# Adding chunk 1 onto chunk 0 for the first block of nodes alone, with twelve tile buffers and GpSimd making layer 1's sender column

## The chip, the cores and the metric

The kernel runs on one core of a Trainium2 chip. The metric is the device time of one execution in microseconds (us). A core has a matrix engine (TensorE, PE in the profile; its weight loads are PEld), three engines for elementwise work (VectorE, DVE; ScalarE, ACT; GpSimd, POOL) and an engine that here only issues DMAs (SyncE, SP). Each engine runs its own list of instructions in order. Where an instruction needs another engine's result, it waits on a semaphore.

## The reference

64 graphs of 256 nodes with 128 features go through four layers; every layer first normalises the rows (layer norm, then ReLU) and adds its result to its input. All of it is float32. The four layers are a pairwise attention (layer 0), a message network with a sigmoid edge weight (layer 1), a dense attention (layer 2) and a gated recurrence of five steps (layer 3). The change touches layer 0 and one column of layer 1:

```python
# layer 0, per graph: W1, W2 are the two halves of adj
s1 = jnp.einsum('bkf,ef->bke', x, W1)
s2 = jnp.einsum('bkf,ef->bke', x, W2)
pre = s1[:, :, None, :] + s2[:, None, :, :] + b_lin
h = jnp.where(pre >= 0, pre, ALPHA * pre)          # ALPHA = 0.2
e = jnp.einsum('bije,e->bij', h, a) + bias         # bias = adj
attn = jax.nn.softmax(e, axis=2)
out = jax.nn.sigmoid(jnp.einsum('bij,bjf->bif', attn, x))
# layer 1
x_h = jax.nn.elu(x @ Wi + bi)
a_src = x_h @ We[:H, 0]
a_tgt = x_h @ We[H:, 0]
e = jax.nn.sigmoid(a_tgt[:, :, None] + a_src[:, None, :] + be[0])
```

For each of the 256 x 256 pairs of nodes of a graph, layer 0 takes a leaky ReLU of 256 sums and their dot product with `a`. That is 64 x 256 x 256 x 256 elements, and it is most of the kernel's work.

## The kernel before

**The pair tiles.** A node i and a chunk `ec` (128 of the 256 entries of `a`) give one tile of 128 partitions (entries of the chunk) x 256 elements (nodes j): the larger of `s2` and minus `s1` of node i. Eight such tiles form a *batch* in a buffer `r` of 128 x 4 x 2 x 256: four groups `g` of 32 nodes by two blocks `ic` of 128 nodes, all for one row t (node `ic*128 + 32*g + t`). The buffers rotate; `BUFS = 11` of them exist. TensorE then multiplies each group of a batch with a window of signs, `a_win`, whose column t selects the row of the output, and sums into `e_ps`, which has the logits of a graph: four matmuls of 512 columns in the program, each on its own 32 columns of the array, so that the four run beside each other. A float32 matmul is two passes in the profile, so a batch is eight MATMUL records.

**Who makes the tiles.** Three engines do, by one line each. VectorE makes four or eight tiles in one instruction (L669, 128x1024 or 128x2048). ScalarE makes one per instruction (L687), and GpSimd one per instruction (L692).

**Merging.** The entries of `a` are sorted by sign and scaled by their absolute value into the weights, so that chunk 0 and chunk 1 have the same sign in each partition, but for one partition at most. So TensorE need not multiply both chunks: VectorE can add chunk 1 of a tile onto its chunk 0 (L709, one instruction that takes the maximum and adds), which is a *merge*. It spares the making of that tile for chunk 1 and TensorE's work on it. A row that is merged needs 8 tiles, 8 merges and one batch; a row that is not needs 16 tiles and two batches. The odd partition is set right by `left2`, `left_w` and `left_b`: `senders` puts a bounded row onto the `adj` bias, for both blocks (`adj_l`, L570), and the softmax adds it (L755).

**What sets the order.** The instruction lists are written by a planner in the kernel (`Model`, `Chain`, and the loop at the end). It keeps a planned time per engine, adds a cost for each instruction (a tile costs ScalarE 365 ns and GpSimd 454, a merge 392, a batch on TensorE 858), and always emits what could start first. Other layers come as chains of steps that interleave with the tiles of the next graphs: `ahead` (layer norm and projections of the next graph), `behind` (softmax of the last graph), `chain12` (layers 1 and 2), `chain3` and later ones (layer 3). `Pairs.begin` decides on a merge by the planner's count: a row is merged where at least `SPARE = 5` finished batches wait for TensorE. The order is fixed when the program is built; the chip runs it with semaphores.

**Groups.** Graphs go in pairs (`GROUPS`: 30 groups of two and four of one). `load_x` fetches a group's input through SyncE into one of five buffers, three groups ahead.

**Layer 1's sender column.** `y_ps` has 129 columns per block, the last being `x_h @ We`. ScalarE copies the first 128 to `y` (L855), and VectorE makes `a_src` of the last out of PSUM, once a graph (L857). The tanh of the edge weights (L875, ScalarE) reads `a_src`.

Of the kernel before, what the change touches and what calls it, by code (L numbers as in the profile page):

```python
# [8 lines left out]
F32 = mybir.dt.float32  # L9
# [3 lines left out]
P = 128  # L13
N = 256
# [4 lines left out]
INV_SQRT_D = 1.0 / (128.0 ** 0.5)  # L19
BUFS = 11  # L20
SPARE = 5
# [34 lines left out]
def kernel(ctx: ExitStack, tc: tile.TileContext, ins: dict, out: bass.AP):  # L56
# [71 lines left out]
    def load_x(g):  # L128
        xt = ap.tile([P, 2 * GROUPS[g], P], F32, tag="xt", name="xt", bufs=5)
        nc.sync.dma_start(out=xt, in_=of_group(x, g))  # L130
        return xt
# [76 lines left out]
    biases = {k: column("L3_gnn_" + k) for k in ("w3_b", "u3_b", "w4_b", "w5_b", "u5_b")}  # L208
    xts.append(load_x(2))

# [9 lines left out]
    def constants0():  # L220
# [32 lines left out]
        dve(2).tensor_tensor(place, dif, neg_pl, ALU.add)  # L253

        last, a_abs1 = col("last"), col("a_abs1")
        dve(2).tensor_scalar(last, place, n_pos, None, ALU.is_equal)
        dve(2).tensor_tensor(a_abs1, a_abs, last, ALU.mult)
        dve(2).tensor_tensor(a_abs1, a_abs, a_abs1, ALU.subtract)
        perm = lent([P, 2, 2, P], "perm", "e_t", 2)
        for src in range(2):  # L260
            for c, size in ((0, a_abs), (1, a_abs1)):
                dve(P).tensor_scalar(
                    perm[:, src, c, :], places[:, c, :], place[:, src : src + 1],
                    size[:, src : src + 1], ALU.is_equal, ALU.mult,
                )
# [43 lines left out]


        odd = constant([P, 1], "odd")
        dve(1).tensor_scalar(odd, p_two[:, 1:2], n_pos, None, ALU.is_equal)
# [7 lines left out]
        dve(2).tensor_tensor(left, a_col, last, ALU.mult)  # L320
        dve(2).tensor_scalar(left, left, odd_all, 0.8, ALU.mult, ALU.mult)
        dve(2).tensor_scalar(left_n, left, -1.0, None, ALU.mult)
# [107 lines left out]
    def ln_relu(space, xt, tag, ln, when=None, at=None):  # L430

        G = xt.shape[1]
        for g in range(G):
            if g % 2 == 0:
                yield "dve", when, at
            if g == 0:
                st = sp.tile([P, G, 6], F32, tag=tag + "_st", name="bst", bufs=2)
                mv = sp.tile([P, G, 2], F32, tag=tag + "_mv", name="bmv", bufs=2)
            dve(P).bn_stats(st[:, g, :], xt[:, g, :])
        yield "dve"  # L440
        for g in range(G):
            dve(6, more=15).bn_aggr(mv[:, g, :], st[:, g, :])
        yield "pool"

        ve = sp.tile([P, G], F32, tag=tag + "_ve", name="bve", bufs=2)
        minus = sp.tile([P, G], F32, tag=tag + "_mm", name="bmm", bufs=2)
        pool(277).tensor_scalar(ve, mv[:, :, 1], 1.0, LN_EPS, ALU.mult, ALU.add)
        pool(150).tensor_scalar(minus, mv[:, :, 0], -1.0, 0.0, ALU.mult, ALU.add)
        rstd = sp.tile([P, G], F32, tag=tag + "_rs", name="brs", bufs=2)
        pool(1085).tensor_tensor(rstd, ve, neg_half[:, 0:G], ALU.pow)  # L450
        shift = sp.tile([P, G], F32, tag=tag + "_sh", name="bsh", bufs=2)
# [81 lines left out]
    def bounds(of):  # L533
# [11 lines left out]
        yield "act"  # L545
        rows = sp.tile([P, P], F32, tag="rows", name="rows", bufs=2)
        act(P, 1).activation(
# [10 lines left out]
    def senders(b, of, to):  # L558

        h_t = flat(of["h_t"][:, 2 * b : 2 * b + 2, :])  # L560
        if "bound" not in of:
            yield from bounds(of)
        yield "pe", settled
        p = psum_h([P, N], "left_ps")
        mm(p, lhsT=left2, rhs=h_t, start=True, stop=True)
        for ic in range(2):
            yield "dve", None, of["bound_at"]
            if ic == 0:
                adj_l = ap.tile([P, 2, N], F32, tag="adj_l", name="adj_l", bufs=3)
            dve(N, 1).scalar_tensor_tensor(  # L570
                adj_l[:, ic, :], p, of["bound"][:, 2 * b + ic : 2 * b + ic + 1], adj_n[:, ic, :],
                ALU.min, ALU.add,
            )
# [12 lines left out]
    class Pairs:  # L586

        def __init__(self, g, b, of, snd):
            self.g, self.b, self.of, self.snd = g, b, of, snd
# [8 lines left out]
                "p c (k g t) -> p c g k t", k=2, g=4  # L601
            )

        def more(self):
# [39 lines left out]

        def nodes(self, t, g2):

            return [
                (g, ic, self.b * N + ic * P + 32 * g + t)
                for g in (2 * g2, 2 * g2 + 1) for ic in range(2)
            ]  # L650

        def make(self, who):
# [10 lines left out]
            if who == "dve":  # L663
                whole = g2 == 0 and self.todo and self.todo[0][0] is batch
                if whole:
                    self.todo.pop(0)
                n = 4 if whole else 2
                model.op("dve", model.WHOLE if whole else model.HALF)
                nc.vector.tensor_tensor(  # L669
                    r[:, 2 * g2 : 2 * g2 + n, :, :],  # L670
                    s2[:, ec : ec + 1, :].unsqueeze(1).to_broadcast([P, n, 2, N]),
                    self.s1n_v[:, ec, 2 * g2 : 2 * g2 + n, :, t : t + 1].to_broadcast([P, n, 2, N]),
                    ALU.max,
# [7 lines left out]
            else:  # L681
                for g, ic, i in self.nodes(t, g2):
                    if g > 2 * g2 or ic:
# [17 lines left out]
        def merge(self):  # L701

            _, batch, g2 = self.merges.pop(0)
            r, t = batch["r"], batch["t"]
            for g, ic, i in self.nodes(t, g2):
                if g > 2 * g2 or ic:
                    yield
# [22 lines left out]
        def multiply(self):  # L730
# [7 lines left out]
            model.op("pe", model.BATCH)  # L738
            for g in range(4):
                nc.tensor.matmul(  # L740
                    self.e_ps[bass.ts(g, 32), :, :].rearrange("p a b -> p (a b)"),
                    lhsT=a_win[:, batch["ec"], 31 - t : 63 - t], rhs=flat(r[:, g, :, :]),
                    start=False, stop=self.over, skip_group_check=True,
                )

    def softmax0(g, b, of, e_ps, snd):
# [87 lines left out]
    def layer1(x1):  # L834
# [8 lines left out]
        for b in range(NB):  # L843
# [11 lines left out]
            act(N).copy(y[:, bass.ts(b, 2), :], y_ps[:, :, 0:P])  # L855
            yield "dve"
            dve(2, 1).tensor_scalar(  # L857
                a_src[:, bass.ts(b, 2)], y_ps[:, :, P], 0.5, be_h, ALU.mult, ALU.add
            )
        yield "pool"  # L860
        x1b = bp.tile([P, G, P], F32, tag="x1b", name="x1b")
        counts["x1"] += 1
# [33 lines left out]
        for b in range(NB):  # L896
            for jc in range(2):
                mm(
                    rc_ps[:, bass.ts(b, N)], lhsT=y[:, b * 2 + jc, :], rhs=e_ts[b][:, jc, :],
                    start=(b == 0 and jc == 0), stop=False, skip_group_check=True,  # L900
                )
# [387 lines left out]
```

## Time and profile before

| What | us |
|---|---|
| time, median of 3 runs | 5038.96 (5033.29 to 5039.40) |
| profiled execution, its own time | 5032.98 |
| span of its profile, first to last instruction | 5031.1 |
| PE busy | 4975.7 |
| PEld busy | 1949.9 |
| DVE busy | 4926.9 |
| ACT busy | 4945.2 |
| POOL busy | 4817.0 |
| last merge on DVE ends at | 4936.5 |

Busy time is the union of an engine's instructions. On PE it says little by itself: a MATMUL record of 512 columns is some 593 ns long, while a set of four starts every 430 ns, so records overlap and cover gaps. What an engine can do at most is better read from the starts of instructions that follow each other without a wait. DMA is busy for 2% of the time, and the granted TensorE clock is 0.999 of full speed.

### The profile page before, as it was taken

The numbers are of one execution on the slowest core, as the hardware profiler recorded it, in microseconds if no ns is written. First come the engines' busy times: TensorE is split into PE (matmuls) and PEld (weight loads), VectorE is DVE, ScalarE is ACT, GpSimd is POOL, SyncE is SP. The second block draws the span as 40 slices with busy tenths as digits, with TensorE's granted clock in tenths as the row PEclk, the third lists the DMA queues.
The fourth block names the chain that finished last, engine by engine and source line by source line (L and its number), as shares of the span: only waits on it lengthen the run. The fifth ranks groups of instructions, "written<-read, shape, count | busy, mean of one in ns | idle before, by whom it ended". The sixth has DMA issues, their size and how long they took to land. (4 is left out here: it accounts for less than half of the span.)

```text
span 5031.1 us, 151796 instructions
## 1 busy us (share of the span) xinstructions
PE 4975.7 (99%) x57307; PEld 1949.9 (39%) x57307; DVE 4926.9 (98%) x9026; ACT 4945.2 (98%) x12984; POOL 4817.0 (96%) x10725
## 2 busy tenths in 40 slices
PE   9999999999999999999999999999999999999998
PEld 3334433333334333343333333333333443333433
DVE  9999999999999999999999999999999999999995
ACT  8999999999999999999999999999999999999995
POOL 8999999999999999999999999999999999999991
PEclk9999999999999999999999999999999999999999
DMA  0000000000000000000000000000000000000000
GB/s 23 4 5 2 5 6 6 6 2 6 6 6 6 2 6 6 6 6 2 6 6 6 6 2 6 6 6 6 4 6 6 6 4 3 5 4 4 4 4 8
DMA packets 56017, 28.02 MB, mean 6 GB/s; under 512 B 20336, under 2 KB 55280, under 8 KB 55280
## 3 DMA queue, kind: packets, MB, share of 16 engines
q1 hardware_dynamic: 54736, 18.04, 1.5%
q8 instruction: 449, 7.36, 0.6%
q14 instruction: 288, 2.36, 0.2%
q10 hardware_dynamic: 544, 0.26, 0.0%
HBM read 9.84 MB, written 8.45 MB: 4 GB/s over the span
## 5 line engine op out<-in xcount | busy, mean ns | idle before, releaser
L692 POOL TENSOR_SCALAR r<-s,s1n 128x256 f32<-128x256 f32 x10100 | 4567.7, 476 | 55.7 <-PE e_ps L740 28.0
L687 ACT ACTIVATE r<-s_act,s 128x256 f32<-128x256 f32 x9736 | 4360.0, 1073 | 4.6 <-PE e_ps L740 4.3
L740 PE MATMUL e_ps<-r,a_win 128*32 128x512 f32 x27824 | 3251.8, 593 | 8.8 <-DVE r L709 4.0
L669 DVE TENSOR_TENSOR r<-s_ps,s1n 128x2048 f32<-128x2048 f32 (+1 forms) x1210 | 2120.7, 1790 | 0.8 <-POOL r L692 0.8
L709 DVE SCALAR_TENSOR_TENSOR r<-s_ps,s1n,r 128x256 f32<-128x256 f32 x4944 | 2013.3, 471 | 0.2
L740 PEld LDWEIGHTS e_ps<-r,a_win 128*32 128x32 f32 x27824 | 918.8, 110 | 1721.4 <-issue 1290.3
L687 ACT ACTIVATE r<-s,s 128x256 f32<-128x256 f32 x512 | 318.8, 1234 | 0.0
L458 ACT ACTIVATE h<-x,bsh,brs 128x128 f32<-128x128 f32 x384 | 264.3, 1040 | 10.5 <-POOL bsh L452 5.0
L109 PE MATMUL m_ps<-adj_t,hn 128*32 128x256 f32 x4096 | 253.6, 381 | 1.1 <-ACT hn L1066 1.1
L1025 ACT ACTIVATE m_ps<-gate_ps,br 128x512 f32<-128x512 f32 (+1 forms) x170 | 194.7, 1145 | 14.2 <-PE gate_ps L109 13.1
L1045 ACT ACTIVATE hv_ps<-hv_ps,bh 128x512 f32<-128x512 f32 (+1 forms) x170 | 198.7, 1169 | 7.2 <-PE hv_ps L109 7.2
L1043 ACT ACTIVATE gate_ps<-gate_ps,bz 128x512 f32<-128x512 f32 (+1 forms) x170 | 203.8, 1200 | 1.1 <-PE gate_ps L109 1.1
L1015 ACT COPY m_t<-m_ps 128x512 f32<-128x512 f32 (+1 forms) x170 | 193.9, 1140 | 6.1 <-PE m_ps L109 5.6
L109 PEld LDWEIGHTS m_ps<-adj_t,hn 128*32 128x32 f32 x4096 | 140.0, 110 | 126.2 <-issue 46.1
L109 PE MATMUL gate_ps<-m_t,t_w_w 128*32 128x512 f32 (+1 forms) x1360 | 172.7, 572 | 2.6 <-ACT m_t L1015 2.2
L109 PE MATMUL gate_ps<-m_t,w_t 128*32 128x512 f32 (+1 forms) x1360 | 172.5, 568 | 2.5 <-ACT m_ps L1025 2.4
L109 PE MATMUL hv_ps<-rh,u_th 128*32 128x512 f32 (+1 forms) x1360 | 172.1, 567 | 2.1 <-DVE rh L1028 2.0
L109 PE MATMUL hv_ps<-m_t,t_w_w 128*32 128x512 f32 (+1 forms) x1360 | 172.4, 568 | 0.0
L1066 ACT COPY hn<-hn_ps 128x512 f32<-128x512 f32 (+1 forms) x136 | 153.2, 1127 | 8.7 <-PE hn_ps L116 8.6
L109 PE MATMUL gate_ps<-hf,u_t 128*32 128x512 f32 (+1 forms) x1088 | 141.9, 571 | 0.0
L109 PE MATMUL s_ps<-h0t,w_p 128*32 128x256 f32 (+1 forms) x1568 | 136.2, 446 | 1.2 <-ACT h0t L474 0.5
L450 POOL TENSOR_TENSOR brs<-bve,neg_half 128x4 f32<-128x4 f32 (+1 forms) x136 | 133.5, 982 | 0.0
(214 smaller groups left out, 4781.2 us busy)
## 6 DMA issues: line engine op xcount, KB each, us to landing
xt<-in_x_dram SPq DMA_DIRECT2D x30, 256.0 KB
out_dram<-y SPq DMA_DIRECT2D x30, 256.0 KB
row<-rows SPq DMA_DIRECT2D x128, 0.5 KB
xt<-in_x_dram SPq DMA_DIRECT2D x4, 128.0 KB
out_dram<-y SPq DMA_DIRECT2D x4, 128.0 KB
bound<-row SPq DMA_DIRECT2D x30, 2.0 KB
raw_L_gnn_w_w<-in_L_gnn_w_w_dram SPq DMA_DIRECT2D x3, 128.0 KB
adj_n<-in_adj_dram ACTq DMA_DIRECT2D x1, 256.0 KB
```

Of the source, the lines that this page charges most:

```text
L109: nc.tensor.matmul(out[bass.ts(c, 32), :], lhsT=lhsT[:, bass.ts(c, 32)], rhs=rhs, **flags)
L458: act(P, 2, 1).activation(h[:, g, :], xt[:, g, :], AF.Relu, bias=shift[:, g : g + 1], scale=rstd[:, g : g + 1],)
L669: nc.vector.tensor_tensor(r[:, 2 * g2 : 2 * g2 + n, :, :], s2[:, ec : ec + 1, :].unsqueeze(1).to_broadcast([P, n, 2, N]), self.s1n_v[:, ec ...
L687: nc.scalar.activation(r[:, g, ic, :], s2[:, ec, :], AF.Relu, bias=s1[:, ec, i : i + 1])
L692: nc.gpsimd.tensor_scalar(r[:, g, ic, :], s2[:, ec, :], FLT_MAX, s1n[:, ec, i : i + 1], ALU.min, ALU.max,)
L709: nc.vector.scalar_tensor_tensor(r[:, g, ic, :], self.own("dve")[:, 1, :], self.of["s1n"][:, 1, i : i + 1], r[:, g, ic, :], ALU.max, ALU.add,)
L740: nc.tensor.matmul(self.e_ps[bass.ts(g, 32), :, :].rearrange("p a b -> p (a b)"), lhsT=a_win[:, batch["ec"], 31 - t : 63 - t], rhs=flat(r[ ...
L1015: act(W).copy(m_t, m_ps)
L1025: act(W, 1).activation(t_r, g_ps, AF.Tanh, bias=br, scale=0.5)
L1043: act(W, 1).activation(t_z, g_ps, AF.Tanh, bias=bz, scale=0.5)
L1045: act(W, 1).activation(cand, hv_ps, AF.Tanh, bias=bh)
L1066: act(W).copy(hn, tp)
```

## The change

Four things change together.

A merged unit is now two rows t and t+1. Chunk 0 of both is made in two batches, and chunk 1 is added onto the tiles of block 0 alone (4 merges per batch instead of 8). Chunk 1 of block 1 of both rows is made as a third batch, marked `two`. So a unit of two rows has 24 tiles, 8 merges and three batches.

Chunk 1 of block 0 now always takes chunk 0's sign, and the left-over entry is set right for block 0 alone (its factor goes from 0.8 to 1.6, and `a_abs1` goes away). Block 1 uses the true signs, so its bias is the plain `adj`, and `adj_l` is made by one VectorE instruction per graph instead of two. Since the two blocks of a chunk-1 batch now need different windows, TensorE multiplies such a batch by eight matmuls of 256 columns instead of four of 512.

`a_src` is made by GpSimd from `y`, which ScalarE now copies with all 129 columns, once a group instead of once a graph.

There are twelve tile buffers instead of eleven; room for them comes from four input buffers instead of five (loads go out two groups ahead), single instead of double buffers for layer norm's small tiles and for `rows`, and an `adj_l` of half the size.

```diff
-BUFS = 11
+BUFS = 12
...
-        xt = ap.tile([P, 2 * GROUPS[g], P], F32, tag="xt", name="xt", bufs=5)
+        xt = ap.tile([P, 2 * GROUPS[g], P], F32, tag="xt", name="xt", bufs=4)
...
-        dve(2).tensor_scalar(left, left, odd_all, 0.8, ALU.mult, ALU.mult)
+        dve(2).tensor_scalar(left, left, odd_all, 1.6, ALU.mult, ALU.mult)
...
-        rstd = sp.tile([P, G], F32, tag=tag + "_rs", name="brs", bufs=2)
+        rstd = sp.tile([P, G], F32, tag=tag + "_rs", name="brs", bufs=1)
...
-        rows = sp.tile([P, P], F32, tag="rows", name="rows", bufs=2)
+        rows = sp.tile([P, P], F32, tag="rows", name="rows", bufs=1)
...
-        for ic in range(2):
-            yield "dve", None, of["bound_at"]
-            if ic == 0:
-                adj_l = ap.tile([P, 2, N], F32, tag="adj_l", name="adj_l", bufs=3)
-            dve(N, 1).scalar_tensor_tensor(
-                adj_l[:, ic, :], p, of["bound"][:, 2 * b + ic : 2 * b + ic + 1], adj_n[:, ic, :],
-                ALU.min, ALU.add,
-            )
+        yield "dve", None, of["bound_at"]
+        adj_l = ap.tile([P, N], F32, tag="adj_l", name="adj_l", bufs=3)
+        dve(N, 1).scalar_tensor_tensor(
+            adj_l, p, of["bound"][:, 2 * b : 2 * b + 1], adj_n[:, 0, :], ALU.min, ALU.add
+        )
...
-            merged = waiting >= SPARE
-            for ec in range(1 if merged else 2):
-                batch = {"t": self.row, "ec": ec, "merged": merged, "halves": 0, "ready": 0.0}
+            merged = waiting >= SPARE and self.row < 31
+            t = self.row
+
+            if merged:
+                kinds = ((t, 0, True, False), (t + 1, 0, True, False), (t, 1, False, True))
+            else:
+                kinds = ((t, 0, False, False), (t, 1, False, False))
+            for t, ec, on_top, two in kinds:
+                batch = {
+                    "t": t, "ec": ec, "merged": on_top, "two": two, "halves": 0, "ready": 0.0
+                }
                 self.todo += [(batch, ec, 0), (batch, ec, 1)]
-            self.row += 1
+            self.row += 2 if merged else 1
...
-            for g, ic, i in self.nodes(t, g2):
-                if g > 2 * g2 or ic:
+            r = batch["r"]
+            for g, ic, i in self.nodes(batch, g2):
+                if ic:
+                    continue
+                if g > 2 * g2:
                     yield
                 model.op("dve", model.MERGE)
...
-            for g in range(4):
-                nc.tensor.matmul(
-                    self.e_ps[bass.ts(g, 32), :, :].rearrange("p a b -> p (a b)"),
-                    lhsT=a_win[:, batch["ec"], 31 - t : 63 - t], rhs=flat(r[:, g, :, :]),
-                    start=False, stop=self.over, skip_group_check=True,
-                )
+
+            if batch["two"]:
+                parts = ((1, t, 1, 0), (1, t + 1, 1, 1))
+            elif batch["ec"]:
+                parts = ((0, t, 0, 0), (1, t, 1, 1))
+            else:
+                parts = ((slice(0, 2), t, 0, slice(0, 2)),)
+            for ic, t, sign, k in parts:
+                for g in range(4):
+                    to, of = self.e_ps[bass.ts(g, 32), ic, :], r[:, g, k, :]
+                    if len(parts) == 1:
+                        to, of = to.rearrange("p a b -> p (a b)"), flat(of)
+                    nc.tensor.matmul(
+                        to, lhsT=a_win[:, sign, 31 - t : 63 - t], rhs=of,
+                        start=False, stop=self.over, skip_group_check=True,
+                    )
...
-                e_ps[:, ic, :], e_ps[:, ic, :], snd["adj_l"][:, ic, :], -1.0, FLT_MAX,
+                e_ps[:, ic, :], e_ps[:, ic, :], adj_n[:, 1, :] if ic else snd["adj_l"], -1.0, FLT_MAX,
...
-                y = bp.tile([P, G, P], F32, tag="y1", name="y1")
-                a_src = sp.tile([P, G], F32, tag="a_src", name="a_src")
-            act(N).copy(y[:, bass.ts(b, 2), :], y_ps[:, :, 0:P])
-            yield "dve"
-            dve(2, 1).tensor_scalar(
-                a_src[:, bass.ts(b, 2)], y_ps[:, :, P], 0.5, be_h, ALU.mult, ALU.add
-            )
+                y = bp.tile([P, G, P + 1], F32, tag="y1", name="y1")
+            act(N + 2).copy(y[:, bass.ts(b, 2), :], y_ps)
         yield "pool"
+        a_src = sp.tile([P, G], F32, tag="a_src", name="a_src")
+        pool(280).tensor_scalar(a_src, y[:, :, P], 0.5, be_h, ALU.mult, ALU.add)
...
-            if g + 3 < len(GROUPS):
-                xts.append(load_x(g + 3))
+            if g + 2 < len(GROUPS):
+                xts.append(load_x(g + 2))
```

More of the change, by code (lines that the diff above doesn't have):

```diff
@@ L208 @@
     biases = {k: column("L3_gnn_" + k) for k in ("w3_b", "u3_b", "w4_b", "w5_b", "u5_b")}
-    xts.append(load_x(2))
     adj_t = constant([P, 2, N], "adj_t")
@@ L253, in constants0 @@
         dve(2).tensor_tensor(place, dif, neg_pl, ALU.add)
-        last, a_abs1 = col("last"), col("a_abs1")
+        last = col("last")
         dve(2).tensor_scalar(last, place, n_pos, None, ALU.is_equal)
-        dve(2).tensor_tensor(a_abs1, a_abs, last, ALU.mult)
-        dve(2).tensor_tensor(a_abs1, a_abs, a_abs1, ALU.subtract)
         perm = lent([P, 2, 2, P], "perm", "e_t", 2)
         for src in range(2):
-            for c, size in ((0, a_abs), (1, a_abs1)):
+            for c in range(2):
                 dve(P).tensor_scalar(
                     perm[:, src, c, :], places[:, c, :], place[:, src : src + 1],
-                    size[:, src : src + 1], ALU.is_equal, ALU.mult,
+                    a_abs[:, src : src + 1], ALU.is_equal, ALU.mult,
                 )
@@ L436, in ln_relu @@
             if g == 0:
-                st = sp.tile([P, G, 6], F32, tag=tag + "_st", name="bst", bufs=2)
-                mv = sp.tile([P, G, 2], F32, tag=tag + "_mv", name="bmv", bufs=2)
+                st = sp.tile([P, G, 6], F32, tag=tag + "_st", name="bst", bufs=1)
+                mv = sp.tile([P, G, 2], F32, tag=tag + "_mv", name="bmv", bufs=1)
             dve(P).bn_stats(st[:, g, :], xt[:, g, :])
@@ L443, in ln_relu @@
         yield "pool"
-        ve = sp.tile([P, G], F32, tag=tag + "_ve", name="bve", bufs=2)
-        minus = sp.tile([P, G], F32, tag=tag + "_mm", name="bmm", bufs=2)
+        ve = sp.tile([P, G], F32, tag=tag + "_ve", name="bve", bufs=1)
+        minus = sp.tile([P, G], F32, tag=tag + "_mm", name="bmm", bufs=1)
         pool(277).tensor_scalar(ve, mv[:, :, 1], 1.0, LN_EPS, ALU.mult, ALU.add)
         pool(150).tensor_scalar(minus, mv[:, :, 0], -1.0, 0.0, ALU.mult, ALU.add)
-        rstd = sp.tile([P, G], F32, tag=tag + "_rs", name="brs", bufs=2)
+        rstd = sp.tile([P, G], F32, tag=tag + "_rs", name="brs", bufs=1)
         pool(1085).tensor_tensor(rstd, ve, neg_half[:, 0:G], ALU.pow)
-        shift = sp.tile([P, G], F32, tag=tag + "_sh", name="bsh", bufs=2)
+        shift = sp.tile([P, G], F32, tag=tag + "_sh", name="bsh", bufs=1)
         pool(302).tensor_tensor(shift, minus, rstd, ALU.mult)
@@ L602, in __init__ @@
             )
+            self.s1n_b = of["s1n"][:, :, bass.ts(b, N)].rearrange(
+                "p c (k g t) -> p c k g t", k=2, g=4
+            )
         def more(self):
@@ L643, in whole, with nodes @@
             batch["ready"] = max(batch["ready"], model.t[who] + LAG[who])
-        def nodes(self, t, g2):
+        def nodes(self, batch, g2):
+            t, two = batch["t"], batch["two"]
             return [
-                (g, ic, self.b * N + ic * P + 32 * g + t)
-                for g in (2 * g2, 2 * g2 + 1) for ic in range(2)
+                (g, k, self.b * N + 32 * g + t + (P + k if two else k * P))
+                for g in (2 * g2, 2 * g2 + 1) for k in range(2)
             ]
@@ L667, in make @@
                 n = 4 if whole else 2
+                if batch["two"]:
+                    s1n = self.s1n_b[:, ec, 1, 2 * g2 : 2 * g2 + n, t : t + 2].unsqueeze(3)
+                else:
+                    s1n = self.s1n_v[:, ec, 2 * g2 : 2 * g2 + n, :, t : t + 1]
                 model.op("dve", model.WHOLE if whole else model.HALF)
@@ L671, in make @@
                     s2[:, ec : ec + 1, :].unsqueeze(1).to_broadcast([P, n, 2, N]),
-                    self.s1n_v[:, ec, 2 * g2 : 2 * g2 + n, :, t : t + 1].to_broadcast([P, n, 2, N]),
+                    s1n.to_broadcast([P, n, 2, N]),
                     ALU.max,
@@ L703, in merge @@
             _, batch, g2 = self.merges.pop(0)
-            r, t = batch["r"], batch["t"]
-            for g, ic, i in self.nodes(t, g2):
-                if g > 2 * g2 or ic:
+            r = batch["r"]
+            for g, ic, i in self.nodes(batch, g2):
+                if ic:
+                    continue
+                if g > 2 * g2:
                     yield
@@ L738, in multiply @@
             model.op("pe", model.BATCH)
-            for g in range(4):
-                nc.tensor.matmul(
-                    self.e_ps[bass.ts(g, 32), :, :].rearrange("p a b -> p (a b)"),
-                    lhsT=a_win[:, batch["ec"], 31 - t : 63 - t], rhs=flat(r[:, g, :, :]),
-                    start=False, stop=self.over, skip_group_check=True,
-                )
+            if batch["two"]:
+                parts = ((1, t, 1, 0), (1, t + 1, 1, 1))
+            elif batch["ec"]:
+                parts = ((0, t, 0, 0), (1, t, 1, 1))
+            else:
+                parts = ((slice(0, 2), t, 0, slice(0, 2)),)
[7 more added lines that the diff above has]
+                        start=False, stop=self.over, skip_group_check=True,
+                    )
     def softmax0(g, b, of, e_ps, snd):
@@ L898, in layer1 @@
                 mm(
-                    rc_ps[:, bass.ts(b, N)], lhsT=y[:, b * 2 + jc, :], rhs=e_ts[b][:, jc, :],
+                    rc_ps[:, bass.ts(b, N)], lhsT=y[:, b * 2 + jc, 0:P], rhs=e_ts[b][:, jc, :],
                     start=(b == 0 and jc == 0), stop=False, skip_group_check=True,
```

## The prediction

> **What bounds the kernel now.** I read the busy shares first, then the groups of instructions with shapes kept apart, then stretches of the timeline for what one instruction really takes, then the waits, and last the busy times of the last 100 us.
>
> ```profile
> PE 4975.7 (99%) x57307; PEld 1949.9 (39%) x57307; DVE 4926.9 (98%) x9026; ACT 4945.2 (98%) x12984; POOL 4817.0 (96%) x10725
> ```
> All four engines are busy nearly all the time, so no single wait is to be hunted: what counts is how much work each engine has, and how much idle time is left on each.
>
> ```profile
> L692 POOL TENSOR_SCALAR r<-s,s1n 128x256 f32<-128x256 f32 x10100 | 4567.7, 476 | 55.7 <-PE e_ps L740 28.0 <-DVE v_rep L303 10.3 <-ACT e_ps L794 1.7
> L687 ACT ACTIVATE r<-s_act,s 128x256 f32<-128x256 f32 x9736 | 4360.0, 1073 | 4.6 <-PE e_ps L740 4.3 <-POOL r L692 0.2
> L740 PE MATMUL e_ps<-r,a_win 128*32 128x512 f32 x27824 | 3251.8, 593 | 8.8 <-DVE r L709 4.0 <-DVE r L669 2.0 <-DVE wn L390 1.7
> L709 DVE SCALAR_TENSOR_TENSOR r<-s_ps,s1n,r 128x256 f32<-128x256 f32 x4944 | 2013.3, 471 | 0.2
> L669 DVE TENSOR_TENSOR r<-s_ps,s1n 128x2048 f32<-128x2048 f32 x659 | 1486.4, 2276 | 0.8 <-POOL r L692 0.8
> L669 DVE TENSOR_TENSOR r<-s_ps,s1n 128x1024 f32<-128x1024 f32 x551 | 652.1, 1209 | 0.0
> L570 DVE SCALAR_TENSOR_TENSOR adj_l<-left_ps,bound,adj_n 128x256 f32<-128x256 f32 x128 | 60.5, 474 | 7.8 <-PE left_ps L109 7.3
> L857 DVE TENSOR_SCALAR a_src<-y_ps,be_h 128x2 f32<-128x2 f32 x64 | 13.3, 208 | 1.9 <-ACT y L855 1.9
> ```
> The makers hardly wait for buffers (POOL 28.0 us and ACT 4.3 us for PE). 27824 records are 3478 batches; 4944 merges are 618 merged rows.
>
> The means overlap their successors, so I take prices from start to start.
>
> ```profile
> 2002.64 2.27 DVE L669 TENSOR_TENSOR r<-s_ps,s1n 128x2048 f32<-128x2048 f32 x1
> 2004.83 0.37 DVE L442 BATCH_NORM_AGGREGATE bmv<-bst 128x2 f32<-128x6 f32 x4
> ...
> 2009.56 3.22 DVE L709 SCALAR_TENSOR_TENSOR r<-s_ps,s1n,r 128x256 f32<-128x256 f32 x8
> 2012.69 1.22 DVE L669 TENSOR_TENSOR r<-s_ps,s1n 128x1024 f32<-128x1024 f32 x1
> ```
> Eight tiles in one VectorE instruction take 2.20 us, a merge 3.13/8 = 0.392, and four tiles (the group's 1.209 less the same 0.08 overlap) 1.13. In the same way a ScalarE tile is 0.356 and a GpSimd tile 0.451 (medians from start to start).
>
> ```profile
> 2003.23 0.13 PEld L740 LDWEIGHTS e_ps<-r,a_win 128*32 128x32 f32 x4 [0.30 <-issue]
> 2003.66 0.13 PEld L109 LDWEIGHTS m_ps<-adj_t,hn 128*32 128x32 f32 x4 [0.30 <-issue]
> 2004.09 1.43 PEld L109 LDWEIGHTS m_ps<-adj_t,hn 128*32 128x32 f32 x28 [0.30 <-issue]
> 2005.60 0.35 PEld L109 LDWEIGHTS gate_ps<-hf,u_t 128*32 128x32 f32 x8
> ```
> Four weight loads go with four matmuls that run beside each other. With 512 columns such a set recurs every 0.43 us (0.429 at the median). With 256 columns seven sets take 2005.60 - 2004.09 = 1.51, 0.216 each. So two half-width sets cost 0.432 against 0.429.
>
> From that I make PE's ledger, which the 99% hides. The pair matmuls need 27824/4 x 0.429 = 2984.1 us; the layers' matmuls 772.2 at 512 columns, 661.8 at 256 and 232.3 at 128 and 129; transposes 154.7; the rest 1.7; together 4806.8. What is left of PE's time is 717 changes between four-tile matmuls and whole-array transposes (99.5, 0.11 us at the median) and 117.7 of other gaps between a set's due start and its real one. Between 50 and 4900 us these gaps are 90.5: about 29 in gaps under 0.1 us each, which come with every such wait, and 61 in real stalls.
>
> ```profile
> PEld e_ps L740 <- DVE r L709: 56.7, 160, 2.7
> POOL r L692 <- PE e_ps L740: 28.0, 18, 4.0
> ```
> The 56.7 is mostly hidden behind running matmuls; of the 61 us, 28.7 stand between two batches, and 13.6 before `left_ps`, which waits for VectorE to release a bank. Makers' own excess over their prices in the same stretch is some 52 us on DVE, 107 on ACT, 66 on POOL. So before, VectorE is the tightest, and PE has 61 us (1.2%) to give.
>
> ```profile
> 4923.00:4938.00 15.00, 15.00 (x195) 6.65 (x191) 13.74 (x38) 6.17 (x13) 1.25 (x4) 1.00 0.01 3
> 4938.00:5031.10 93.10, 74.85 (x1044) 35.39 (x1035) 35.65 (x88) 39.09 (x92) 4.42 (x14) 0.96 0.03 7
> ```
> (Columns: length, then busy time and instructions of PE, PEld, DVE, ACT, POOL, clock, DMA.) At the end VectorE merges alone for 12 us, and a chain of 93 us through the last graph's layers follows.
>
> **The change, part by part.** Counts are those of the two built programs.
>
> *Merges and tiles.* Merges fall from 4944 to 4520; tiles rise from 27824 to 28248, batches from 3478 to 3531. VectorE: -424 x 0.392 = -166.2, +60 x 2.198 = +131.9, +34 x 1.131 = +38.5, so +4.2. ScalarE: 84 tiles fewer, -29.9. GpSimd: 108 fewer, -48.7.
>
> *adj_l.* 64 fewer at 0.392: -25.1 on DVE. Their PE source is unchanged.
>
> *a_src.* VectorE loses 64 x 0.127 (start to start) = -8.1. GpSimd gains 34; nearest row is its 128x4 `bve` at 0.277, so +9.4, with 0.2 to 0.5 each as ends (7 to 17). ScalarE's copy grows by two columns in 256, at 0.3 us a copy under 0.2 us in all. The new wait is the tanh (L875) behind GpSimd's tiles. Behind it on ScalarE stand its tiles, but in the steady part the chain step is placed after it; if cover fails, a GpSimd tile (0.45) per group, 15 us. I take nothing; ends 0 and 15. In the tail GpSimd is idle.
>
> Sums: DVE -29.0, ACT -29.8, POOL -39.3.
>
> *PE.* 2048 batches stay 512 wide; the 1483 of chunk 1 become two halves. 2048 x 0.858 + 1483 x 0.864 = 3038.5 against 2984.1: +54.4, of which 53 more batches are 45.5 and halving 8.9. Instruction order puts 4.1 us of PE's work behind the last pair matmul that was ahead of it; there PE idles, so the steady part gets +50.3.
>
> Half-width sets also double the weight loads: 1483 x 2 more sets x 0.13 us = 386 us of loads. In the 256-wide stretch above the loads run side by side with the matmuls, 0.216 per set, so I take nothing. The Trainium skill, "TensorE: Matmul & The Clock Gate", section "Part 3: Packing small matmuls — row/col tiling", says a weight load overlaps a running matmul only in other rows of the array; all of these use the same 128 rows, so by it the 386 us would be exposed and the time some 5425. The trace differs: 0.216 a set with its loads.
>
> *Buffers.* The twelfth buffer lets 8 more tiles wait: it bears on GpSimd's 28.0 and ScalarE's 4.3 (ends: -32 idle, or none). These engines are not the last ones then, so nothing.
>
> *Inputs and small tiles.* The SP queue issues a load two groups ahead instead of three. A group is some 155 us apart from the next, and the DMAs are 2% busy, so it lands long before; it passes the `row` and `bound` DMAs (0.5 and 2 KB) only. Single small buffers are reused a group later. At the start, where groups 0 and 1 come close together, each may cost one wait; 0 to 4 us, taken as 0, as the startup holds 10 us of PE gaps already. Constants lose three tiny DVE instructions: below 0.5 us.
>
> *The sum.* The makers get 29 to 39 us lighter, but PE gets 50.3 heavier in a stretch where only 61 us of stalls can be removed. The run can't end sooner than PE allows: 50.3 - 61 = -10.7 with no stall left. I take 17 us left (the 13.6 before `left_ps`, whose bank is no tile buffer, and a little between batches): 50.3 - 44 = +6.3. Ends: none left, -10.7; all left, +50.3. On the profiled execution's 5032.98 that is 5039; the runs' median stands 6.0 above it, so 5038.96 + 6.3 = 5045.
>
> **The rivals.**
>
> *A, PE takes over (0.55).* 7 to 30 us of stalls stay: 5035 to 5058. For it: makers that are ahead fill the buffers, and single groups of the trace already run with under 1 us of PE gaps in 155 us. Against it: nothing shows the whole run so.
>
> *B, the makers still set the end (0.20).* PE absorbs the batches: stalls vanish and half of the 29 us of small gaps is only the shadow of late tiles. Then 50.3 - 61 - 14.5 = -25, next to VectorE's -29: about 5014, range 5010 to 5035. For it: PE's waits name late tiles. Against it: small gaps stand before transposes too, where no tile is late. The Trainium skill, "Perfetto Trace Analysis", section "Identifying the Most-Contended Engine", says matmul busy time misjudges PE and weight-load busy share should be used; here that is 39%, which would leave PE wide open and give VectorE's -29, 5010. The trace bears out the first half only: sets at 0.43 us leave no room though loads are busy for 0.13 of it.
>
> *C, the stalls stay (0.25), slower.* The order is fixed, so a late batch holds PE up though others are ready. If stalls are made by the order and not by a shortage of tiles, over 30 of 61 us stay: 5058 to 5089. It decides from about 21 us of remaining stalls on (+10). For it: at 85% of the batch starts another finished batch was waiting, and yet there are stalls. Against it: that stall needs a late maker, and makers get lighter. The exposed weight loads (5425) have under 0.01 of this.
>
> That the merging isn't done as said is ruled out by the counts.
>
> **How the numbers follow.** 0.2% is 10 us, about what a measurement of this kernel can tell from no change. B lies below 5029 in 0.18; A within 5029 to 5049 in 0.42, with 0.02 of B; the rest of A (0.13) and C (0.25) above. The range goes from the middle of B to near C's end, 5018 to 5085; A alone is 5035 to 5058.
>
> **What would show it.** DVE's sum down 29 us and its idle up; pair matmuls in two forms, half-width sets at 0.216 apart; POOL's and ACT's waits for `e_ps` well above 28 and 4 us (A); PE's large gaps at 10 to 30 us (A), near 60 (C), near none with unchanged maker waits (B). I am wrong if half-width sets take longer than 0.22, or if `a_src` or a load shows among the long waits.

## The result, and the profile after

The changed kernel takes 5023.99 us (median of 8 runs, 5020.27 to 5026.66) against 5038.92 us of the kernel before on the same chip: the ratio is 0.997, with a 95% interval of 0.996 to 0.998. Two repetitions beside the experiments below gave 0.9978 (0.9969 to 0.9988) and 0.9976 (0.9967 to 0.9986). So it is faster by 0.2 to 0.3%, 11 to 15 us. The forecast was 5045 us, a change within 0.2%, with "faster" at 0.18. The range of 5018 to 5085 holds the time, but the direction was missed. The time lies in the range of rival B (5010 to 5035, chance 0.20), and outside that of A (5035 to 5058, 0.55).

The profiled execution took 5023.80 us, its span is 5022.0 us: 9.1 us below the span before. The busy shares and the pair work of the changed kernel (the page's first part, then groups with shapes kept apart):

```profile
PE 4986.5 (99%) x69595; PEld 2287.9 (46%) x69595; DVE 4900.4 (98%) x8566; ACT 4924.1 (98%) x12900; POOL 4798.7 (96%) x10651
```
```profile
L703 POOL TENSOR_SCALAR r<-s,s1n 128x256 f32<-128x256 f32 x9992 | 4539.2, 508 | 72.4 <-PE e_ps L764 37.2 <-DVE v_rep L299 9.7 <-issue 5.8
L698 ACT ACTIVATE r<-s_act,s 128x256 f32<-128x256 f32 x9652 | 4268.3, 971 | 11.2 <-PE e_ps L764 11.0
L764 PE MATMUL e_ps<-r,a_win 128*32 128x512 f32 x16384 | 2039.0, 593 | 2.6 <-DVE r L680 2.6
L722 DVE SCALAR_TENSOR_TENSOR r<-s_ps,s1n,r 128x256 f32<-128x256 f32 x4520 | 1854.8, 471 | 1.3 <-POOL r L703 0.9
L764 PE MATMUL e_ps<-r,a_win 128*32 128x256 f32 x23728 | 1529.5, 380 | 1.6 <-DVE r L680 1.4
L565 DVE SCALAR_TENSOR_TENSOR adj_l<-left_ps,bound,adj_n 128x256 f32<-128x256 f32 x64 | 30.4, 474 | 5.8 <-PE left_ps L109 5.6
```
Every maker is less busy (VectorE by 26.5 us, ScalarE by 21.1, GpSimd by 18.3), PE a little more. The pair matmuls come in the two widths, the makers wait longer for PE to free a buffer (POOL 37.2 us after 28.0, ACT 11.0 after 4.3). TensorE's weight loads wait less for late merges than before, when they waited 56.7 us for them (time, count and median):

```profile
PEld e_ps L764 <- DVE r L722: 24.0, 81, 0.3
```

Half-width sets in a stretch of the weight loads (start, length, engine, line):

```profile
1002.16 0.13 PEld L764 LDWEIGHTS e_ps<-r,a_win 128*32 128x32 f32 x4 [0.30 <-issue]
1002.59 0.56 PEld L764 LDWEIGHTS e_ps<-r,a_win 128*32 128x32 f32 x12 [0.30 <-issue]
1003.24 0.35 PEld L109 LDWEIGHTS gate_ps<-m_t,t_w_w 128*32 128x32 f32 x8
```
Three sets of loads in 0.65 us: 0.216 each, also at the median of all 5932 such sets (23728 records by four). The doubled loads cost nothing, as forecast.

The same ledger of PE from the starts of its matmuls, before and after:

| us | before | after |
|---|---|---|
| needed by the matmuls and transposes | 4806.8 | 4861.2 |
| changes to and from transposes, 717 each | 99.5 | 84.3 |
| other gaps, 50 to 4900 us | 90.5 | 45.8 |
| other gaps, start and end | 27.2 | 23.1 |

All gaps together fall from 217.2 to 153.2 us, by 64.0, while PE needs 54.4 more. That sum can be relied on. How it is split over the rows hangs on which of the four matmuls of a set is taken as its start, since the four don't always start together: with the first one the changes fall from 112.8 to 86.0, with the last from 88.9 to 83.6, and the rest of the 64 us lies in the other rows.

And the last stretch of the changed kernel (length, then busy time and instructions of PE, PEld, DVE, ACT, POOL, clock, DMA):

```profile
4850.00:4911.20 61.20, 61.12 (x786) 25.82 (x782) 60.36 (x132) 60.42 (x159) 58.76 (x134) 1.00 0.01 3
4911.20:4926.10 14.90, 14.82 (x212) 6.45 (x204) 2.16 (x5) 3.65 (x6) 0.67 (x2) 1.00 0.05 14
4926.10:5022.00 95.90, 78.17 (x1108) 37.90 (x1108) 38.32 (x94) 41.73 (x98) 5.97 (x19) 0.95 0.03 7
```
All three makers end together near 4911 (before: 4923, 4925 and VectorE at 4936.5), and PE works off finished batches for 15 us more. Before, PE ended its pair matmuls 1 us behind VectorE, at 4937.6. So the makers gained 11 to 25 us, and PE's backlog and a closing chain that is some 2.5 us longer take part of it back.

### The profile page after: what moved, and what is told of

Its sections match the earlier page's. It is cut to its first block, busy times and chain, and to the rows that moved or that the text cites. A ratio compares the mean times of both kernels' runs of the same rounds, so it can differ in the third digit from the quotient of the medians.

```text
span 5022.0 us, 175964 instructions
## 1 busy us (share of the span) xinstructions
PE 4986.5 (99%) x69595; PEld 2287.9 (46%) x69595; DVE 4900.4 (98%) x8566; ACT 4924.1 (98%) x12900; POOL 4798.7 (96%) x10651
## 4 chain that ended last, share of the span: by engine, by line
PE 84%; ACT 8%; DVE 6%; POOL 1%; issue 1%; DMA 0%; DVEq 0%; ACTq 0%; POOLq 0%
PE e_ps L764 51%; PE gate_ps L109 7%; ACT r L698 6%; PE hv_ps L109 5%; PE m_ps L109 5%; PE s_ps L109 3%; DVE r L680 3%; PE o_ps L109 2%; PE e_ps L109 2%; PE rc_ps L109 1%; DVE r L722 1%; PE hn_ps L116 1%; PE rsum_ps L109 1%; POOL r L703 1%; PE e_ps L116 1%
## 5 line engine op out<-in xcount | busy, mean ns | idle before, releaser
L703 POOL TENSOR_SCALAR r<-s,s1n 128x256 f32<-128x256 f32 x9992 | 4539.2, 508 | 72.4 <-PE e_ps L764 37.2
L698 ACT ACTIVATE r<-s_act,s 128x256 f32<-128x256 f32 x9652 | 4268.3, 971 | 11.2 <-PE e_ps L764 11.0
L764 PE MATMUL e_ps<-r,a_win 128*32 128x256 f32 (+1 forms) x40112 | 3255.6, 467 | 4.2 <-DVE r L680 4.0
L680 DVE TENSOR_TENSOR r<-s_ps,s1n 128x2048 f32<-128x2048 f32 (+1 forms) x1304 | 2297.2, 1797 | 3.1 <-PE e_ps L764 2.8
L764 PEld LDWEIGHTS e_ps<-r,a_win 128*32 128x32 f32 x40112 | 1278.3, 110 | 1581.5 <-issue 874.7
L722 DVE SCALAR_TENSOR_TENSOR r<-s_ps,s1n,r 128x256 f32<-128x256 f32 x4520 | 1854.8, 471 | 1.3 <-POOL r L703 0.9
L698 ACT ACTIVATE r<-s,s 128x256 f32<-128x256 f32 x512 | 301.0, 1123 | 0.0
L455 ACT ACTIVATE h<-x,bsh,brs 128x128 f32<-128x128 f32 x384 | 236.4, 902 | 6.7 <-POOL bsh L449 6.1
L1063 ACT ACTIVATE gate_ps<-gate_ps,bz 128x512 f32<-128x512 f32 (+1 forms) x170 | 186.8, 1099 | 2.7 <-PE gate_ps L109 2.7
L1035 ACT COPY m_t<-m_ps 128x512 f32<-128x512 f32 (+1 forms) x170 | 177.2, 1042 | 4.3 <-PE m_ps L109 4.3
```

Source lines behind the costliest of these rows:

```text
L455: act(P, 2, 1).activation(h[:, g, :], xt[:, g, :], AF.Relu, bias=shift[:, g : g + 1], scale=rstd[:, g : g + 1],)
L680: nc.vector.tensor_tensor(r[:, 2 * g2 : 2 * g2 + n, :, :], s2[:, ec : ec + 1, :].unsqueeze(1).to_broadcast([P, n, 2, N]), s1n.to_broadcast ...
L698: nc.scalar.activation(r[:, g, ic, :], s2[:, ec, :], AF.Relu, bias=s1[:, ec, i : i + 1])
L703: nc.gpsimd.tensor_scalar(r[:, g, ic, :], s2[:, ec, :], FLT_MAX, s1n[:, ec, i : i + 1], ALU.min, ALU.max,)
L722: nc.vector.scalar_tensor_tensor(r[:, g, ic, :], self.own("dve")[:, 1, :], self.of["s1n"][:, 1, i : i + 1], r[:, g, ic, :], ALU.max, ALU.add,)
L764: nc.tensor.matmul(to, lhsT=a_win[:, sign, 31 - t : 63 - t], rhs=of, start=False, stop=self.over, skip_group_check=True,)
```

## The experiments

Each run's time is a median, and the ratio is to the kernel before on the same chip. The median of the kernel before itself was 5032 us on some chips and 5039 to 5041 on others, so ratios and marks of the same level are compared. The mark of the changed kernel is 5020.57 and 5019.65 us where the kernel before took 5032, and 5023.99 where it took 5039. The mark was not always taken on the chip of the run that is held against it, so a difference of 1 or 2 us from a mark says nothing.

| run | us | kernel before | ratio (95%) |
|---|---|---|---|
| after_again | 5020.57 | 5031.70 | 0.9978 (0.9969 to 0.9988) |
| after_mark | 5019.65 | 5031.99 | 0.9976 (0.9967 to 0.9986) |
| after_pe_load | 5039.92 | 5032.30 | 1.0015 (1.0005 to 1.0024) |
| before_pe_load | 5039.74 | 5032.30 | 1.0015 (1.0006 to 1.0025) |
| after_dve_load | 5025.92 | 5032.30 | 0.9989 (0.9979 to 0.9998) |
| after_pe_less | 5017.27 | 5039.15 | 0.9955 (0.9940 to 0.9970) |
| before_pe_less | 5035.95 | 5039.15 | 0.9993 (0.9983 to 1.0002) |
| after_dve_less | 5021.42 | 5039.15 | 0.9963 (0.9949 to 0.9977) |
| before_dve_less | 5038.82 | 5039.15 | 0.9999 (0.9990 to 1.0009) |
| after_11_buffers | 5026.62 | 5032.30 | 0.9988 (0.9979 to 0.9998) |
| merge_alone | 5022.89 | 5031.70 | 0.9984 (0.9974 to 0.9993) |
| after_spare4 | 5020.38 | 5031.70 | 0.9976 (0.9966 to 0.9986) |
| before_new_order | 5032.07 | 5031.70 | 1.0002 (0.9992 to 1.0011) |
| before_even_end | 5041.08 | 5031.99 | 1.0019 (1.0009 to 1.0028) |
| before_spare6 | 5032.55 | 5031.99 | 1.0001 (0.9992 to 1.0010) |
| after_late_merges | 5019.06 | 5031.99 | 0.9974 (0.9964 to 0.9984) |
| before_half_adj | 5026.09 | 5040.60 | 0.9972 (0.9961 to 0.9983) |
| before_s6_half_adj | 5028.41 | 5040.60 | 0.9976 (0.9966 to 0.9985) |

The first two are the changed kernel unaltered, as the mark for the runs beside it.

> The changed kernel itself, unaltered, as the mark for the other runs on this chip: 0.997 of the kernel before, as measured first (0.996 to 0.998).

> The changed kernel, unaltered, as the mark for the runs beside it: 0.996 to 0.998 of the kernel before.

### Which engine sets the end: loads put on and taken off

The theory at this point was that PE had become the bound; the rival, that the makers set the end in both kernels. A load that the planner does not know of leaves the order as it is. The runs `after_pe_load` and `before_pe_load` put four matmuls with zero weights (`zero_w`) behind every 64th batch:

```diff
             model.op("pe", model.BATCH)
+            counts["batch"] += 1
+            if counts["batch"] % 64 == 0 and not self.over:
+                for g in range(4):
+                    nc.tensor.matmul(
+                        self.e_ps[bass.ts(g, 32), 0, :], lhsT=zero_w, rhs=r[:, g, 0, :],
+                        start=False, stop=False, skip_group_check=True,
+                    )
```


> The changed kernel with 55 extra sets of four 256-column matmuls with zero weights (one set behind every 64th batch, in two passes of 0.216 us: 55 x 0.432 = 23.8 us of PE work), which the planner does not know of; nothing else moves and the values stay the same. Theory 1 (after the change PE sets the end; before, the makers of the tiles did, with PE room to spare): PE has only some 17 to 27 us of removable stalls left, so most of the load shows: 14 to 24 us longer than the changed kernel, 5038 to 5048. Theory 2 (the makers set the end in both): 0 to 8 us longer, 5024 to 5032.

> The kernel before with the same extra load: 54 sets of four 256-column matmuls with zero weights behind every 64th batch, 23.3 us of PE work unknown to the planner. Theory 1 (makers set the end here, PE has some 86 us of removable stalls): it is swallowed but for 0 to 8 us, 5039 to 5047. Theory 3 (PE set the end before as well): 15 to 23 us longer, 5054 to 5062.

In the changed kernel the load cost 19 us against its mark; in the kernel before 7.4 us. PE's ledger shows 22.5 us more needed in the first and 22.0 in the second; in the second the gaps gave way (117.7 to 104.5), in the first they could hardly (65 to 68.9 in executions without the load, 61.2 with it). Theory 1 holds for work that is added to PE. The waits of the makers in the changed kernel with the load:

```profile
POOL r L705 <- PE e_ps L773: 49.4, 24, 5.4
ACT r L700 <- PE e_ps L773: 13.6, 19, 2.8
```
With more PE work GpSimd waits for buffers longer still (37.2 to 39.3 us without the load).

The run `after_dve_load` adds work to VectorE:

```diff
         dve(N, 1).scalar_tensor_tensor(
             adj_l, p, of["bound"][:, 2 * b : 2 * b + 1], adj_n[:, 0, :], ALU.min, ALU.add
         )
+        nc.vector.scalar_tensor_tensor(
+            adj_l, p, of["bound"][:, 2 * b : 2 * b + 1], adj_n[:, 0, :], ALU.min, ALU.add
+        )
```


> The changed kernel with the adj_l instruction issued twice per graph, the second writing the same values: 64 x 0.392 = 25.1 us more on VectorE, which the planner does not know of. Theory 1 (PE sets the end): VectorE, 29 us lighter than before and idle while PE works off the batches, swallows it: 0 to 6 us longer than the changed kernel. Theory 2 (the makers set the end): 18 to 25 us longer, 5042 to 5049.

It cost 5 to 6 us of 25.1: VectorE has room in the changed kernel, so VectorE alone does not set its end.

Then the same engines were made lighter. PE first, in `after_pe_less` and `before_pe_less`:

```diff
-                rhs=wm[:, 0, :], start=True, stop=False
-            )
-            mm(
-                o1_ps[:, g, :], lhsT=xh_t[:, bass.ts(g, P)], rhs=wm[:, 1, :], start=False, stop=True
-            )
+                rhs=wm[:, 0, :], start=True, stop=True
+            )
+            model.op("pe", P * 1.676)
```


> The changed kernel without layer 1's second matmul into o1_ps (the part of the output that multiplies x_h with the second half of Wm is left out): 128 times a 128-column matmul of two passes of 0.110 us, 28.2 us of PE work fewer, with the planner's cost kept, so that all else stands in the same order and no wait goes. Theory 1 (PE alone sets the end): 18 to 28 us shorter than the changed kernel. Theory 4 (PE and the makers are level; whichever gets heavier sets the end, and neither alone can shorten it): 0 to 8 us shorter.

> The kernel before without the same matmul (the same part of the output left out, the planner's cost kept): 28.2 us of PE work fewer. Makers set the end there, so 0 to 6 us shorter than the kernel before; if PE set it, 18 to 28 us shorter.

6.7 us shorter than the changed kernel's 5023.99, and 3.2 us shorter than the kernel before, out of 28.2. Theory 1 in its plain form falls: with less PE work the changed kernel's gaps grow (86.4 us after 68.9) and the makers set the end. PE and the makers are level in it, and only work that is added to PE shows nearly in full.

Then VectorE, in `after_dve_less`:

```diff
-        adj_l = ap.tile([P, N], F32, tag="adj_l", name="adj_l", bufs=3)
-        dve(N, 1).scalar_tensor_tensor(
-            adj_l, p, of["bound"][:, 2 * b : 2 * b + 1], adj_n[:, 0, :], ALU.min, ALU.add
-        )
+        adj_l = adj_n[:, 0, :]
+        dve(N, 1)
```


> The changed kernel without the adj_l instruction (the correction of the odd entry in block 0's logits is left out and the plain adj is used), the planner's cost kept: 64 x 0.392 = 25.1 us fewer on VectorE. Theory 1 and theory 4: 0 to 4 us shorter. Theory 2 (the makers set the end): 10 to 25 us shorter.

And in `before_dve_less`:

```diff
+            if ic:
+                dve(N, 1)
+                continue
             dve(N, 1).scalar_tensor_tensor(
...
-                e_ps[:, ic, :], e_ps[:, ic, :], snd["adj_l"][:, ic, :], -1.0, FLT_MAX,
+                e_ps[:, ic, :], e_ps[:, ic, :], adj_n[:, 1, :] if ic else snd["adj_l"][:, 0, :], -1.0, FLT_MAX,
```


> The kernel before without the adj_l instruction of block 1 (its correction of the odd entry is left out and the plain adj is used), the planner's cost kept: 25.1 us fewer on VectorE, which is what the change takes off by the same step. If VectorE is the tightest of the makers, with ScalarE and GpSimd some 50 us of excess behind it: 6 to 18 us shorter than the kernel before. If all three makers are level: 0 to 6 us.

2.6 us and 0.3 us shorter: 25 us off VectorE alone are worth little or nothing in either kernel. The first outcome that was expected for the kernel before (VectorE the tightest, 6 to 18 us) did not come; the second did. That fits makers that are level; that they are so because the planner shares the tiles out is an explanation that no run tests by itself.

### Which part of the change brings the time

`after_11_buffers`:

```diff
-BUFS = 12
+BUFS = 11
```


> The changed kernel with eleven tile buffers; the planner writes a new order, with the same 4520 merges. If the twelfth buffer is what took the stalls off PE, they come back: 5033 to 5045. If the unit of three batches with four merges each is what did, the time stays within 4 us of the changed kernel's: 5020 to 5028.

0.9988: 5 to 7 us above the marks. The twelfth buffer is worth some 0.1% of the time in this order, about half of the gain and not the whole. GpSimd's wait for `e_ps` is 63.2 us in it, after 37.2 to 39.3 with twelve buffers.

`merge_alone`:

```diff
-BUFS = 12
+BUFS = 11
...
-                y = bp.tile([P, G, P + 1], F32, tag="y1", name="y1")
-            act(N + 2).copy(y[:, bass.ts(b, 2), :], y_ps)
+                y = bp.tile([P, G, P], F32, tag="y1", name="y1")
+                a_src = sp.tile([P, G], F32, tag="a_src", name="a_src")
+            act(N).copy(y[:, bass.ts(b, 2), :], y_ps[:, :, 0:P])
+            yield "dve"
+            dve(2, 1).tensor_scalar(
+                a_src[:, bass.ts(b, 2)], y_ps[:, :, P], 0.5, be_h, ALU.mult, ALU.add
+            )
         yield "pool"
-        a_src = sp.tile([P, G], F32, tag="a_src", name="a_src")
-        pool(280).tensor_scalar(a_src, y[:, :, P], 0.5, be_h, ALU.mult, ALU.add)
...
```


> The new merged unit alone: the changed kernel with eleven tile buffers and with the sender column made by VectorE out of PSUM as before. The planner makes 4472 merges (48 fewer than in the changed kernel), so 6 more batches: 5.1 us more on PE. Theory 1 (PE sets the end, and the smoother unit is what keeps PE fed): 3 to 15 us longer than the changed kernel, still no longer than the kernel before. Rival (the twelfth buffer and GpSimd's column bring the gain): the kernel before's time or up to 10 us above it.

0.9984, 2.3 us above the mark: the merged unit, with the `adj_l` instruction that it spares, brings most of it, and together with the run above, GpSimd's column brings nothing that can be measured. This run has eleven buffers too and yet comes closer to the mark than the run above, in another order. So what the twelfth buffer is worth is known only as some 2 to 7 us, and the order alone may make a few us.

`after_spare4`:

```diff
-SPARE = 5
+SPARE = 4
```


> The changed kernel with SPARE = 4, so that rows are merged when four finished batches wait instead of five: 4752 merges (232 more), 29 batches fewer. PE gets 29 x 0.858 = 24.9 us lighter; VectorE 232 x 0.392 - 33 x 2.198 - 8 x 1.131 = 9.4 us heavier, GpSimd 32 x 0.451 = 14.4, ScalarE 32 x 0.356 = 11.4. Theory 1 (PE sets the end): 6 to 14 us shorter than the changed kernel, until the makers bind. Theory 2 (the makers set the end): 9 to 14 us longer.

No change (5020.38 against 5020.57). PE needs 25 us less, its gaps and changes grow by the same 25.6 us, and the makers end 7 us later. It is the same level as above, seen from the planner's side: neither theory's number came.

`before_new_order`:

```diff
-LAG = {"pe": 300, "dve": 150, "act": 170, "pool": 200}
+LAG = {"pe": 300, "dve": 160, "act": 170, "pool": 200}
```


> The kernel before with one number of its planner changed (the assumed delay behind VectorE 160 ns instead of 150): the work is the same but for 8 merges more, the order of the instructions is written anew. If the 0.3% gain of the change is the luck of a rewritten order, such a rewriting moves the time by 8 us or more in either direction. If it is the work and the bound, the time stays within 4 us of the kernel before.

1.0002: one rewritten order did not move the time.

### Is it the uneven end, the number of merges, or the correction?

`before_even_end`:

```diff
-            merged = waiting >= SPARE
+            merged = waiting >= SPARE and not (self.g == len(GROUPS) - 1 and self.row >= 16)
```


> The kernel before, with no merges in the second half of the last graph (rows 16 to 31), so that VectorE does not merge alone for 12 us at the end; 80 merges fewer, 10 batches more on PE (8.6 us), the rest of the order as before. If the uneven end is what the change repairs: 6 to 11 us shorter than the kernel before. If the gain comes from the whole run: 0 to 3 us shorter.

9 us longer, a miss: VectorE did end its tiles earlier (4930.7), but PE's last pair matmul moved from 4937.6 to 4945.0. The uneven end was not a loss to be repaired.

`after_late_merges`:

```diff
-            merged = waiting >= SPARE and self.row < 31
+            merged = waiting >= (0 if self.g >= len(GROUPS) - 1 else SPARE) and self.row < 31
```


> The changed kernel, with every row of the last graph merged, so that PE has less to work off behind the makers, who end 15 us ahead of it: 16 merges more, 2 batches fewer. Theory 4 (PE and makers level, with PE's backlog at the end on the path): 1 to 5 us shorter than the changed kernel. If the backlog is only a consequence of the chain behind it: the same within 1 us.

0.6 us shorter than the mark beside it: PE's backlog at the end is not what could be saved.

`before_spare6`:

```diff
-SPARE = 5
+SPARE = 6
```


> The kernel before with SPARE = 6: 4640 merges, 304 fewer, near the changed kernel's 4520, with the old unit of one row and eight merges. VectorE 1.9 us lighter, ScalarE 18.5, GpSimd 30.7; PE 38 batches, 32.6 us heavier. If fewer merges alone bring the gain: 6 to 12 us shorter than the kernel before. If the old unit can't keep PE fed at that load: within 4 us of it, or longer.

1.0001. In the kernel before, PE takes 32.6 us more and its gaps and changes shrink by 33, as in the changed kernel. So the old unit keeps PE fed as well, and yet there is no gain, though ScalarE has 18.5 us less to do and GpSimd 30.7; VectorE's own work is 1.9 us lighter only. That left the `adj_l` instruction, half of whose uses the new unit makes unnecessary. In the last two runs, `before_half_adj` and `before_s6_half_adj`, the kernel before leaves it out for block 1, and the planner knows it. The second has `SPARE = 6` besides.

```diff
+            if ic:
+                continue
             dve(N, 1).scalar_tensor_tensor(
...
-                e_ps[:, ic, :], e_ps[:, ic, :], snd["adj_l"][:, ic, :], -1.0, FLT_MAX,
+                e_ps[:, ic, :], e_ps[:, ic, :], adj_n[:, 1, :] if ic else snd["adj_l"][:, 0, :], -1.0, FLT_MAX,
```


> The kernel before without the adj_l instruction of block 1 (its correction of the odd entry is left out), and now the planner knows it and writes a new order: 88 merges more, 11 batches fewer. VectorE 8.6 us lighter, ScalarE 8.5, GpSimd 1.8, PE 9.4. If what VectorE saves is worth something once it is spread over the engines: 4 to 9 us shorter than the kernel before. If not: within 3 us.

> The same with SPARE = 6: the old unit of one row and eight merges, with the saving of block 1's adj_l spread and 28 batches more on PE than before (24.0 us). VectorE 12.3 us lighter, ScalarE 24.2, GpSimd 34.3. If the gain of the change is the saved adj_l spread over the makers while PE takes more batches, in whichever unit: 6 to 11 us shorter than the kernel before. If the new unit is needed to keep PE fed at that load: within 4 us of it.

0.9972 and 0.9976: as much as the whole gain, with the old unit, eleven buffers and VectorE's column. Luck of a rewritten order is an unlikely reason: two rewritten orders with the full correction (`before_new_order`, `before_spare6`) gave 1.0002 and 1.0001. The busy shares and the pair work of the first:

```profile
PE 4972.3 (99%) x57219; PEld 1926.1 (38%) x57219; DVE 4918.5 (98%) x9019; ACT 4943.2 (98%) x12960; POOL 4835.3 (96%) x10721
```
```profile
L694 POOL TENSOR_SCALAR r<-s,s1n 128x256 f32<-128x256 f32 x10096 | 4587.9, 534 | 40.9 <-PE e_ps L742 13.2 <-DVE v_rep L303 10.1 <-DVE x L972 1.8
L711 DVE SCALAR_TENSOR_TENSOR r<-s_ps,s1n,r 128x256 f32<-128x256 f32 x5032 | 2050.1, 472 | 0.0
```
Here VectorE's free time went into 88 more merges, which make PE lighter; with `SPARE = 6` it went into tiles, and PE got heavier. The time is the same within 2.3 us. So the mechanism, as far as the runs show it: the four engines are level, a saving on one is worth nothing where it stands (`before_dve_less`, 0.3 us), and about as much as the whole change once the planner has spread it (`before_half_adj`, 14.5 us). So the likely reading is that the new unit is itself no faster than the old, and brings time because it allows the correction of block 1 to go. This part is argued: the new unit with the full correction kept, which would show it directly, was not run.

What stays open is the size. If a saving is spread evenly, a quarter of the sum over the four engines should show. The counts give this, beside what was measured:

| run | sum over the engines, us | a quarter | measured |
|---|---|---|---|
| the change | -43.7 | -10.9 | -14.9 (marks: -11.1, -12.3) |
| before_half_adj | -28.3 | -7.1 | -14.5 |
| before_s6_half_adj | -46.8 | -11.7 | -12.2 |
| before_spare6 | -18.5 | -4.6 | +0.6 |
| after_spare4 | +10.3 | +2.6 | -0.2 |

The quarter has the direction wherever the time moved clearly, and the change's own quarter could have been worked out from the prediction's four sums. But it misses three of the five by 3 to 7 us, so it is no law.

## Why the prediction was wrong, step by step

**Wrong: the size of what PE can give.** The ledger's needs were right: +54.4 us was forecast and stands in the trace. The failed step is the size of the gaps that can go: "PE gets 50.3 heavier in a stretch where only 61 us of stalls can be removed", of which 17 were to stay. So 44 us of gaps were to go, and 4.1 more at the end. In the trace all gaps together fell by 64.0, some 16 us more than these 48.1. The forecast for the span was +6.3 and it moved by -9.1, which is nearly the same difference.

By the split that the prediction used, the 44 came nearly as forecast (90.5 to 45.8), and the excess lies in the term beside it, "717 changes between four-tile matmuls and whole-array transposes (99.5, 0.11 us at the median)", which was counted as fixed. It fell to 84.3. Gaps over 0.15 us at such changes held 33.8 us in 82 of them before, and 12.9 us in 25 after. With the part of them above the median some 86 us could be removed, and not 61. The split is less sure than the sum: with the last matmul of each set as its start, only 5 of the 64 us lie at the changes, and then it is the 44 that was too small (98.9 to 43.8).

What stands before the transposes is mostly not their own wait. With the first matmul as the start of a set, 59 of 83 such gaps over 0.15 us follow a set whose four matmuls started over 0.06 us apart, where an undisturbed set takes 0.02. Such staggered sets are 1136 of 15391 before and 196 of 18463 after. One of the longest, in the weight loads of the kernel before (the last line is the transpose):

```profile
4286.01 0.14 PEld L740 LDWEIGHTS e_ps<-r,a_win 128*32 128x32 f32 x2 [0.65 <-DVE r L709]
4286.79 0.14 PEld L740 LDWEIGHTS e_ps<-r,a_win 128*32 128x32 f32 x2 [0.65 <-DVE r L709]
4288.18 0.14 PEld L740 LDWEIGHTS e_ps<-r,a_win 128*32 128x32 f32 x2 [1.24 <-DVE r L709]
4289.15 0.20 PEld L116 LDWEIGHTS y_ps<-ident,hf 128*128 128x128 f32 x2 [0.84 <-issue]
```
Here the groups of one batch come one by one, each when VectorE has merged it. What made the other sets stagger was not sorted.

**Wrong: the offset.** I put the median 6.0 us above the profiled execution for the changed kernel too. That execution of the kernel before was at the low end of its runs, that of the changed kernel was at its median (5023.80 and 5023.99). So the medians are 15 apart where the spans are 9.

**Half right: PE takes over.** Added PE work shows (19 us of 22.5 needed, against 7.4 before), and GpSimd's and ScalarE's waits for `e_ps` rose, though GpSimd's not "well above" its 28 us. PE's gaps over 0.1 us came to 16 us, within A's 10 to 30. But less PE work brought 6.7 of 28.2, so PE is level with the makers and not the bound by itself. The step "The run can't end sooner than PE allows" stands; what PE allowed was put 16 us too high.

**Wrong as a reading of the kernel before: VectorE the tightest.** Taking 25 us from it changed the time by 0.3 us. That fits makers that were all level.

**Right.** Merges, tiles, half-width sets (0.216), hidden weight loads, `a_src` (0.23 us from start to start where 0.277 was taken; its longest wait, 8.3 us, falls at the end) and the input loads cost what was said or less.

**Set at nothing, and not nothing: the twelfth buffer.** It is worth some 2 to 7 us, inside its bounds (-32 to none), and so may be a good part of the 21 us between forecast and time.

**Rival B** had the direction, and its reason was wrong in the place it named: gaps under 0.1 us between 50 and 4900 us did not shrink (23 us before, 25 after, with the first matmul of a set as its start). What shrank were long gaps, those before transposes among them. The makers' waits, which B had unchanged, rose.

## What to carry to other kernels

Where a planner has levelled the engines, the price of an instruction on its own engine is no forecast: taken off without a new plan it was worth 0.3 us here, with a new plan 14.5. Add up the change over all engines as well: a quarter of that sum had the direction here (-10.9 us), which the look at one bounding engine had not, though it missed single runs by up to 7 us. Test a cause with both kinds of run, with the plan kept and with it made anew. And when gaps are sorted into fixed and removable ones, look at the spread of each kind: a median of 0.11 us hid 25 us of long gaps in 82 of 717.
